# Five polynomial rounds instead of six, whole-tile ring places, one load for each slot

## The chip, the cores and the metric

The kernel runs on one core of one Trainium2 chip. The metric is the device time of one execution in microseconds (us). Three runs of the kernel before took 4946.76, 4948.24 and 4950.79 us, so the median is 4948.24 us.

## The reference: what is computed

The input `x` has 32 images of 64 channels and 56 by 56 = 3136 pixels. The work has two layers.

Layer 0 is a polynomial of the channels. The 64 channels are 8 groups of 8. In each group every product of two channels (36 of them) and of three channels (120) is formed at each pixel, and each set of products is mixed by a small matrix:

```
p2 = x[:, :, _I2] * x[:, :, _J2]
y2 = einsum('bgihw,goi->bgohw', p2, W2) + b2
p3 = x[:, :, _I3] * x[:, :, _J3] * x[:, :, _K3]
y3 = einsum('bgihw,goi->bgohw', p3, W3) + b3
return inp + y2 * beta2 + y3 * beta3 * 0.1
```

Layer 1 takes the result `l` of each image, `theta` being its first 32 channels. It forms the 3136 by 3136 matrix `theta^T theta`, takes a softmax of it along one axis and a second softmax of the result along the other, and multiplies this into `g = clip(bn(w_inside l), 0, 6)`. A 3 by 3 depthwise convolution, a normalization and the addition of `l` end the layer. Everything is float32.

## The kernel before, in words

**Layout.** The host reorders the channels so that the 32 rows of half an image (four groups) come as 8 planes of 4 rows, and appends the first five planes again behind the last. A load that begins `d` planes later therefore holds the channels turned by `d` places within each group. A product of channels `i`, `i+a`, `i+b` is the product of three loads with the offsets 0, `a`, `b`.

**Slots and rounds.** The 128 partitions are four slots of 32 rows. `STEPS` (line 51) says which offset `a` a slot has (slot 0 to 3: 0, 1, 2, 3) and with which `b` its products are extended. In round 0 GpSimd (POOL) forms `q = x0 * xa` for all slots at once; in rounds 1 to 4 it multiplies `q` by the tiles named `0`, `2`, `4` and `b`. TensorE (PE) multiplies each round's tile by its weights `wq[:, r]` and accumulates all rounds in PSUM. The fifth step, the pairs at offset 4, has no extension. It is a round of its own (round 5): POOL multiplies two small loads (`c`, offsets 0 and 4) of all four half images of a chunk in one instruction of 128 by 242, and PE multiplies that by a separate weight tile `w4`.

In the kernel before, the slot is the fast index of the partition (`wq[s::NSLOT]`, line 138), so one DMA with a plane step (`grow` in `LOADS`, line 216) fills all 128 partitions of one half image; only tile `b` needs two.

**Pairs, chunks and units.** Images go in 16 pairs. While the attention of pair `n` runs, the polynomial of pair `n+1` is made in 13 chunks of 242 pixels. A chunk of a pair has four half images (`ks`, four values of `k`). `products` (line 375) is a generator that emits a chunk's POOL instructions; it asks for room in two rings of products, `q` (8 places) and `pr` (20 places), and for loaded inputs. `load_next` and `prefetch` (lines 330 and 362) emit the loads in the order of a plan, as the rings `x0`, `xs` and `xc` have places and a credit of DMAs (`PACE`, line 305, given twice per attention tile) lasts. All loads of `x` behind the prologue are issued by SyncE (SP).

The second image of the first pair is made alone: chunks of two half images and 484 pixels (`TWO`). The first image of the first pair is made in a prologue of seven chunks of 448 pixels (`first_loads`, `first_products`, `first_poly`), where VectorE (DVE) does the multiplying and SP and ScalarE's queue (ACTq) issue the loads in turn.

**The attention's loop.** A pair has 49 tiles of 128 rows (`IT`). In loop step `t` PE makes the scores of tile `t` in two halves (`ps`, one PSUM buffer of four banks), DVE moves each half to SBUF and takes the row minimum (`e<-ps`), ACT makes two exponentials of 3136 columns, and PE multiplies tile `t-3` into the values (`av` and `ax<-gq,e`). The order on every engine is the order in which the program is written (`pin`, line 91). Between the halves there are places for other work, `aux0` and `aux1` for PE: units of the polynomial, each of two rounds (`rounds(..., 2)`, line 923), and units that make `g`. A chunk of a pair has three units, in `aux0` of three tiles that follow each other; `BETWEEN` (line 917) says where `g` units follow. `weight` and `split` divide the `av` products between a tile's two halves by the size of the units. After a chunk's last unit `poly_out` (line 493) adds the bias and `x` (the tile `xc`) on DVE.

## Time and profile before

| what | value |
|---|---|
| profiled execution: its span; the lowest time of the three runs | 4946.9 us; 4946.76 us |
| PE, ACT, DVE, POOL busy | 4722.0, 4553.9, 4120.5, 3208.4 us |
| one pair in the middle (from 3016.33 to 3309.82 us) | 293.49 us, 49 tiles |
| in that pair: PE, ACT, DVE, POOL busy | 287.90, 284.44, 255.94, 208.68 us |
| DMA in that pair | 0.57 of 16 engines, 145 GB/s |
| first exponential | at 124.44 us |

Times are microseconds unless marked ns. In the groups a line gives the engine, the operation, what it writes and reads, the shape and the count, then the busy time of the group, the mean of one instruction in ns, and the idle time ahead of them with what ended it. Every line number is that of a helper (L110), so tiles tell the groups apart. PE runs each float32 product in two passes, so a product is two records.

### The profile page before, as it was taken

What the parts mean: (1) busy time and instruction counts of PE and PEld (TensorE: products, weight loads), DVE (VectorE), ACT (ScalarE), POOL (GpSimd) and SP (SyncE); (2) the same over time, 40 slices, a digit from 0 to 9 for tenths busy, and PEclk for the clock granted to TensorE, in tenths of its full rate; (3) what the DMA queues carried; (4) which work ended last, traced back from release to release, by engine and by line L of the source; (5) the groups of instructions that cost most, each with busy time, mean ns of one, the idle gap of its engine ahead of it and who ended that gap; (6) DMA issues with size and microseconds to landing.
All of it is one profiled execution on the core that took longest, in us unless ns stands there. A gap on an engine that the chain in (4) does not pass through costs nothing.

```text
span 4946.9 us, 263995 instructions
## 1 busy us (share of the span) xinstructions
PE 4722.0 (95%) x118122; PEld 3215.6 (65%) x118122; DVE 4120.5 (83%) x6100; ACT 4553.9 (92%) x2356; POOL 3208.4 (65%) x4275
## 2 busy tenths in 40 slices
PE   4998999999999999999999999999999999999887
PEld 1555666666666666666666666666666666666665
DVE  4655898888988898888889889888888889888887
ACT  0777899999999999999999999999999999999996
POOL 1777685858758586785858768585875858678000
PEclk8999999999999999999999999999999999999999
DMA  6555656565565655556565555656555565554201
GB/s 203 152 148 153 146 144 155 145 151 141 138 145 145 152 147 143 147 145 144 149 145 147 147 146 142 150 145 152 146 140 141 150 147 146 145 147 125 45 11 34
DMA packets 875486, 685.65 MB, mean 139 GB/s; under 512 B 289772, under 2 KB 860524, under 8 KB 870252
## 3 DMA queue, kind: packets, MB, share of 16 engines
q1 hardware_dynamic: 865964, 657.85, 52.0%
q8 instruction: 924, 15.14, 1.3%
q10 hardware_dynamic: 8384, 10.91, 0.7%
q14 instruction: 214, 1.75, 0.1%
HBM read 565.65 MB, written 25.69 MB: 120 GB/s over the span
## 4 chain that ended last, share of the span: by engine, by line
PE 78%; DVE 11%; issue 3%; DMA 3%; ACT 3%; POOL 1%; SPq 1%; ACTq 0%; DVEq 0%; POOLq 0%
PE av L110 33%; PE ps L110 26%; PE ax L110 19%; DVE e L110 9%; ACT e L110 3%; DMA ring_xs<-in_x_dram 2%; POOL ring_pr L110 1%; DVE y L110 1%; DVE num L110 1%; SPq L110 1%; DMA ring_xc<-in_x_dram 1%; DMA first<-in_x_dram 1%; PE first_s L110 0%; DMA th<-y 0%; POOL ring_q L110 0%
## 5 line engine op out<-in xcount | busy, mean ns | idle before, releaser
L110 PEld LDWEIGHTS av<-gq,e 128*64 128x64 f32 x64512 | 2011.4, 138 | 943.1 <-issue 936.1
L110 ACT ACTIVATE e<-e,nm 128x3136 f32<-128x3136 f32 x784 | 2282.9, 2912 | 235.2 <-DVE e L110 219.6
L110 ACT ACTIVATE e<-e,rz 128x3136 f32<-128x3136 f32 x784 | 2270.3, 2896 | 0.0
L110 PE MATMUL av<-gq,e 128*64 128x65 f32 x64512 | 2224.2, 225 | 3.1 <-ACT e L110 3.0
L110 POOL TENSOR_TENSOR ring_pr<-ring_q,ring_xs 128x242 f32<-128x242 f32 (+2 forms) x2382 | 1784.5, 783 | 533.7 <-PE ax L110 522.8
L110 DVE TENSOR_SCALAR_CACHE_REDUCE e<-ps 128x1568 f32<-128x1568 f32 x784 | 1403.8, 1791 | 321.1 <-PE ps L110 301.7
L110 DVE TENSOR_SCALAR_CACHE_REDUCE e<-ps,nm 128x1568 f32<-128x1568 f32 x784 | 1448.3, 1847 | 254.1 <-PE ps L110 249.1
L110 PE MATMUL ps<-th 32*64 32x392 f32 x25088 | 1453.5, 515 | 131.6 <-DVE e L110 112.3
L110 POOL TENSOR_TENSOR ring_pr<-ring_q,ring_x 128x242 f32<-128x242 f32 (+2 forms) x794 | 606.2, 789 | 607.4 <-PE ax L110 574.8
L110 DVE SCALAR_TENSOR_TENSOR y<-tt,wdt,y 128x605 f32<-128x605 f32 (+6 forms) x711 | 708.2, 996 | 6.4 <-DMA tt<-tr 5.2
L110 PEld LDWEIGHTS ps<-th 32*64 32x64 f32 x25088 | 370.4, 130 | 476.8 <-DVE e L110 382.4
L110 POOL TENSOR_TENSOR ring_q<-ring_x,ring_xs 128x242 f32<-128x242 f32 (+2 forms) x794 | 570.3, 745 | 169.3 <-DMA ring_xs<-in_x_dram 166.4
L110 PE MATMUL ax<-gq,e 128*64 128x65 f32 x12288 | 490.3, 222 | 0.0
L110 PE MATMUL ax<-ring_pr,wq 128*32 128x242 f32 (+1 forms) x6448 | 474.5, 373 | 2.2 <-POOL ring_pr L110 1.1
L110 PEld LDWEIGHTS ax<-gq,e 128*64 128x64 f32 x12288 | 425.5, 138 | 0.3
L110 PEld LDWEIGHTS ax<-ring_pr,wq 128*32 128x32 f32 x6448 | 177.0, 109 | 106.9 <-POOL ring_pr L110 13.3
L110 POOL TENSOR_SCALAR y<-y,bias 128x616 f32<-128x616 f32 (+2 forms) x79 | 145.4, 1842 | 98.9 <-PE ax L110 98.9
L110 DVE SCALAR_TENSOR_TENSOR y<-ax,bias,ring_xc 128x242 f32<-128x242 f32 (+3 forms) x208 | 97.0, 467 | 102.6 <-PE ax L110 102.6
L110 PE MATMUL ax<-wit,y 128*64 128x64 f32 x3136 | 143.3, 223 | 31.1 <-issue 17.9
L110 POOL TENSOR_TENSOR ring_pr<-ring_xc 128x242 f32<-128x242 f32 (+3 forms) x208 | 127.7, 615 | 67.8 <-DMA ring_xc<-in_x_dram 59.2
L110 ACT ACTIVATION_READ_ACCUMULATOR e<-e,nm 128x1 f32 x784 | 145.4, 185 | 0.0
L110 PEld LDWEIGHTS ax<-wit,y 128*64 128x64 f32 x3136 | 118.9, 139 | 37.0 <-issue 18.7
(86 smaller groups left out, 1388.4 us busy)
## 6 DMA issues: line engine op xcount, KB each, us to landing
ring_xs<-in_x_dram SPq DMA_DIRECT2D x2184, 121.0 KB
ring_x<-in_x_dram SPq DMA_DIRECT2D x720, 121.0 KB
ring_xs<-in_x_dram SPq DMA_DIRECT2D x1440, 60.5 KB
th<-y SPq DMA_DIRECT2D x124, 392.0 KB
ring_xc<-in_x_dram SPq DMA_DIRECT2D x360, 121.0 KB
ring_xs<-in_x_dram SPq DMA_DIRECT2D x186, 116.0 KB
out_dram<-y SPq DMA_DIRECT2D x60, 308.0 KB
tt<-tr SPq DMA_DIRECT2D x128, 100.0 KB
```

Of the source, the lines that this page charges most:

```text
L110: i = f(*args, **kw)
```

## The change

- `STEPS` gets other extensions, so that round 1 multiplies `q` by the tile `a` itself (offsets 0 to 3), and slot 2 has nothing to do in round 2. Into that free slot go the pairs at offset 4: after the round's four products, four more POOL instructions of 32 partitions by 242 overwrite slot 2 with `x0 * x(offset 4)`. Round 5, `w4` and the second of the two `c` loads go. Five rounds stay; the third unit of a chunk holds one round instead of two.
- The slot becomes the slow index: slot `s` is partitions 32s to 32s+31. A tile of a chunk holds all half images of the chunk, and each of its four slots is filled by one DMA (`slot_loads`), 32 partitions by 4 half images by 242 columns.
- The rings hold whole tiles: `x0` 8 places instead of 6, `xs` 16 instead of 14, `xc` 2 of one load instead of 3 of two. Places come free a tile at a time. `PACE` goes from 4.5 to 4.
- POOL still multiplies one half image in each instruction (`pieces`).
- The prologue is changed in the same way; DVE does the extra slot there.

```
-    (0, [0, 2, 4, 5]),
-    (1, [0, 2, 4, 1]),
-    (2, [0, 2, 4, 5]),
-    (3, [0, 2, 4, 1]),
+    (0, [0, 2, 4, 1]),
+    (1, [1, 3, 4, 2]),
+    (2, [2, 4, 3]),
+    (3, [3, 5, 4, 0]),
     (4, []),
...
+SR, SS = 2, 2
...
     LOADS = {
-        "0": [(0, 1, 0, 0)],
-        "a": [(0, 1, 0, 1)],
-        "2": [(0, 1, 2, 0)],
-        "4": [(0, 1, 4, 0)],
-        "b": [(0, 2, 5, 0), (1, 2, 1, 0)],
+        "0": (0, 0, 0, 0),
+        "a": (0, 1, 2, 3),
+        "2": (2, 3, 4, 5),
+        "4": (4, 4, 4, 4),
+        "b": (1, 2, 3, 0),
     }
+    SPARE = slice(SS * 32, SS * 32 + 32)
+
+    def slot_loads(name, k0, nk, p0, w):
+        for s, d in enumerate(LOADS[name]):
+            yield slice(s * 32, s * 32 + 32), bass.AP(
+                x.tensor, (k0 * EXT + d) * 4 * N + p0, [[N, 32], [EXT * 4 * N, nk], [1, w]]
+            )
...
-    XB = {"x0": 6, "xs": 14, "xc": 3}
+    XB = {"x0": 8, "xs": 16, "xc": 2}
...
-    PACE = 4.5
+    PACE = 4
...
+        def times(dst, a, b):
+            for pc in pieces(ks):
+                pool.tensor_tensor(dst[:, pc, :], a[:, pc, :], b[:, pc, :], ALU.mult)
...
+        q = take_ring("q", w, nk)
+        times(q, x0, xa)
+        prefetch()
+        done(q)
+        for r, of in enumerate("a24b", 1):
+            yield "pr", m * nk
+            if of != "a":
+                yield "load", (n, c, ks, of)
+            xr = xa if of == "a" else use(of)
+            p = take_ring("pr", w, nk)
+            times(p, q, xr)
+            if r == SR:
+                times(p[SPARE], x0[SPARE], xr[SPARE])
+                held["x0"] -= m * nk
+            held["xs"] -= m * nk
             prefetch()
-                for r in range(0, NRND + 1, per)
+                for r in range(0, NRND, per)
```

More of the change, by code (lines that the diff above doesn't have):

```diff
@@ L132, in tile_poly_conv_attention @@
     wq = const.tile([128, NRND, 2, 32], FP, name="wq")
-    w4 = const.tile([128, 128], FP, name="w4")
     at = 0
     for s, (_, bs) in enumerate(STEPS):
-        for h in range(2) if s < NSLOT else ():
-            act.dma_start(
-                out=wq[s::NSLOT, :, h, :],
-                in_=wpoly[h * 32 : h * 32 + 32, at : at + NRND, h * 32 : h * 32 + 32],
-            )
-        if s == NSLOT:
-            act.dma_start(out=w4, in_=wpoly[:, at, :])
+        p0 = (s if s < NSLOT else SS) * 32
+        ranges = [(0, NRND, at)]
+        if s == SS:
+            ranges = [(0, SR, at), (SR + 1, NRND, at + SR)]
+        if s == NSLOT:
+            ranges = [(SR, SR + 1, at)]
+        for r0, r1, a in ranges:
+            for h in range(2):
+                act.dma_start(
+                    out=wq[p0 : p0 + 32, r0:r1, h, :],
+                    in_=wpoly[h * 32 : h * 32 + 32, a : a + r1 - r0, h * 32 : h * 32 + 32],
+                )
         at += 1 + len(bs)
@@ L160, in tile_poly_conv_attention @@
             out=ax[:, k * 256 : k * 256 + 256],
-            lhsT=w4,
+            lhsT=wq.rearrange("p k h o -> p (k h o)")[:, :128],
             rhs=wq.rearrange("p k h o -> p (k h o)")[:, :256],
@@ L204, in tile_poly_conv_attention @@
     firsts = [ep.tile([128, N], FP, name=f"first_{i}", tag="e") for i in range(4)]
-    def parts(tiles):
-        return [t[:, p : p + FW] for t in tiles for p, _ in FCS]
-    fx, fp = parts(firsts), parts(ys[1:] + [tt])
+    fx = [t[:, p : p + 2 * FW].rearrange("p (k w) -> p k w", k=2) for t in firsts for p, _ in FCS[:6:2]]
+    fc = [t[:C, 6 * FW :] for t in firsts]
+    fp = [t[:, p : p + FW] for t in ys[1:] + [tt] for p, _ in FCS]
     fat = {"x": 0, "p": 0, "q": 0, "c": 0}
@@ L216, in tile_poly_conv_attention, with load @@
     LOADS = {
-        "0": [(0, 1, 0, 0)],
-        "a": [(0, 1, 0, 1)],
-        "2": [(0, 1, 2, 0)],
-        "4": [(0, 1, 4, 0)],
-        "b": [(0, 2, 5, 0), (1, 2, 1, 0)],
-    }
+        "0": (0, 0, 0, 0),
[3 more added lines that the diff above has]
+        "b": (1, 2, 3, 0),
+    }
+    SPARE = slice(SS * 32, SS * 32 + 32)
[3 more added lines that the diff above has]
+                x.tensor, (k0 * EXT + d) * 4 * N + p0, [[N, 32], [EXT * 4 * N, nk], [1, w]]
+            )
     def first_loads(c):
         p0, w = FCS[c]
-        def load(dst, k, d, grow, steps):
-            src = bass.AP(x.tensor, (k * EXT + d) * 4 * N + p0, [[N, 32], [grow * 4 * N, steps], [1, w]])
-            if steps == 1:
-                src = bass.AP(x.tensor, (k * EXT + d) * 4 * N + p0, [[N, 32], [1, w]])
+        def load(dst, src):
             (act if fat["q"] % 2 else sync).dma_start(out=dst, in_=src)
@@ L234, in first_loads @@
         fxs[c] = {}
-        for name, k in [(a, k) for k in (0, 1) for a in "0a"] + [(a, k) for a in "24b" for k in (0, 1)]:
+        for name in "0a24b":
             t = fx[fat["x"] % len(fx)]
             fat["x"] += 1
-            fxs[c][name, k] = t
-            for s0, every, d, grow in LOADS[name]:
-                load(t[s0::every, :] if every > 1 else t, k, d, grow, NSLOT // every)
-        for d in (0, 1):
-            t = fx[fat["x"] % len(fx)]
-            fat["x"] += 1
-            fxs[c]["c", d] = t[:C, :]
-            for k in (0, 1):
-                load(t[k * 32 : k * 32 + 32, :], k, 4 * d, 0, 1)
+            for at, src in slot_loads(name, 0, 2, p0, w):
+                load(t[at], src)
+            for k in (0, 1):
+                fxs[c][name, k] = t[:, k, :]
+        t = fc[c % len(fc)]
+        fxs[c]["c"] = t
+        for k in (0, 1):
+            load(t[k * 32 : k * 32 + 32, :], bass.AP(x.tensor, k * EXT * 4 * N + p0, [[N, 32], [1, w]]))
     def first_products(c):
@@ L257, in first_products @@
         q = {k: product(xs["0", k], xs["a", k]) for k in (0, 1)}
-        frs[c] = [q] + [{k: product(q[k], xs[a, k]) for k in (0, 1)} for a in "024b"]
-        dve.tensor_tensor(xs["c", 1], xs["c", 0], xs["c", 1], ALU.mult)
-        frs[c].append(dict.fromkeys((0, 1), xs["c", 1]))
+        frs[c] = [q]
+        for r, a in enumerate("a24b", 1):
+            frs[c].append({})
+            for k in (0, 1):
+                p = product(q[k], xs[a, k])
+                if r == SR:
+                    dve.tensor_tensor(p[SPARE], xs["0", k][SPARE], xs[a, k][SPARE], ALU.mult)
+                frs[c][r][k] = p
     first_loads(0)
@@ L269, in tile_poly_conv_attention @@
     for k in range(NRND):
-        by = row("beta2_0") if k == 0 else b3row
-        w = wq[:, k, :, :].rearrange("p h o -> p (h o)")
-        dve.tensor_tensor(w, w, by, ALU.mult)
-    for half in (0, C):
-        w = w4[:, half : half + C]
-        dve.tensor_tensor(w, w, row("beta2_0"), ALU.mult)
+        cuts = [(slice(0, 128), row("beta2_0") if k == 0 else b3row)]
+        if k == SR:
+            cuts = [
+                (slice(0, SPARE.start), b3row),
+                (SPARE, row("beta2_0")),
+                (slice(SPARE.stop, 128), b3row),
+            ]
+        for at, by in cuts:
+            w = wq[at, k, :, :].rearrange("p h o -> p (h o)")
+            dve.tensor_tensor(w, w, by[at], ALU.mult)
     bias0 = const.tile([128, 1], FP, name="bias0")
@@ L313, in tile_poly_conv_attention @@
     ring = {t: [xp.tile([128, m, PCH], FP, name=f"ring_{t}", tag=t, bufs=1), 0] for t, m in XB.items() if t != "xc"}
-    ringc = xp.tile([128, 2 * XB["xc"] * PCH], FP, name="ring_xc", tag="xc", bufs=1)
+    ringc = xp.tile([128, XB["xc"] * PCH], FP, name="ring_xc", tag="xc", bufs=1)
     def chunks(ks):
@@ L320, in many, with pieces, take_ring @@
         return -(-w // PCH)
-    def take_ring(tag, w):
+    def pieces(ks):
+        return [slice(k, k + 1) for k in range(len(ks))]
+    def take_ring(tag, w, nk=1):
         t, at = ring[tag]
-        m, size = many(w), t.shape[1]
-        if at % m or at + m > size:
+        m, size = many(w) * nk, t.shape[1]
+        at = -(-at // m) * m
+        if at + m > size:
             at = 0
         ring[tag][1] = (at + m) % size
-        return t[:, at : at + m, :].rearrange("p m w -> p (m w)")[:, :w]
+        return t[:, at : at + m, :].rearrange("p (k m) w -> p k (m w)", k=nk)[:, :, :w]
     def load_next():
         tag, key = plan.pop(0)
-        n, c, ks, name, k = key
+        n, c, ks, name = key
         p0, w = chunks(ks)[c]
@@ L337, in load_next @@
             p0, w = p0 + sub * PCH, min(PCH, w - sub * PCH)
-            o = fat["c"] % XB["xc"] * 2 * PCH
+            o = fat["c"] % XB["xc"] * PCH
             fat["c"] += 1
-            t = ringc[:, o : o + 2 * PCH].rearrange("p (d w) -> p d w", d=2)
             at = slice(ks[0] * 32, ks[-1] * 32 + 32)
-            for d in range(2):
-                src = bass.AP(
-                    x.tensor,
-                    ((4 * n + ks[0]) * EXT + 4 * d) * 4 * N + p0,
-                    [[EXT * 4 * N, len(ks)], [N, 32], [1, w]],
-                )
-                start(t[at, d, :w], src)
-            loaded[key] = [t[at, d, :w] for d in range(2)]
-            return
-        held[tag] += many(w)
-        t = take_ring(tag, w)
-        for s0, every, d, grow in LOADS[name]:
             src = bass.AP(
                 x.tensor,
-                ((4 * n + k) * EXT + d) * 4 * N + p0,
-                [[N, 32], [grow * 4 * N, NSLOT // every], [1, w]],
-            )
-            start(t[s0::every, :] if every > 1 else t, src)
+                (4 * n + ks[0]) * EXT * 4 * N + p0,
+                [[EXT * 4 * N, len(ks)], [N, 32], [1, w]],
+            )
+            loaded[key] = ringc[at, o : o + w]
+            start(loaded[key], src)
+            return
+        held[tag] += many(w) * len(ks)
+        t = take_ring(tag, w, len(ks))
+        for at, src in slot_loads(name, 4 * n + ks[0], len(ks), p0, w):
+            start(t[at], src)
         loaded[key] = t
@@ L363, in prefetch @@
         while plan and credit[0] >= 1:
-            tag, (_, c, ks, _, _) = plan[0]
-            m = 1 if tag == "xc" else many(chunks(ks)[c][1])
+            tag, (_, c, ks, _) = plan[0]
+            m = 1 if tag == "xc" else many(chunks(ks)[c][1]) * len(ks)
             if held[tag] + m > XB[tag]:
@@ L380, in products @@
         p0, w = chunks(ks)[c]
-        m = many(w)
-        def use(name, k=None):
-            key = n, c, ks, name, k
-            return loaded.pop(key)
-        x0 = {}
-        rounds = [{}]
+        m, nk = many(w), len(ks)
+        rounds = []
         both = []
         prods[n, c, ks] = rounds, both
-        yield "q", m * len(ks)
-        for k in ks:
-            yield "load", (n, c, ks, "a", k)
-            x0[k] = use("0", k)
-            xa = use("a", k)
-            q = take_ring("q", w)
-            pool.tensor_tensor(q, x0[k], xa, ALU.mult)
-            rounds[0][k] = q
-            held["xs"] -= m
-            prefetch()
@@ L401, in products @@
-        for r, of in enumerate(("0", "2", "4", "b")):
-            rounds.append({})
-            yield "pr", m * len(ks)
-            for k in ks:
-                if of != "0":
-                    yield "load", (n, c, ks, of, k)
-                xr = x0[k] if of == "0" else use(of, k)
-                p = take_ring("pr", w)
-                pool.tensor_tensor(p, rounds[0][k], xr, ALU.mult)
-                rounds[-1][k] = p
-                held["x0" if of == "0" else "xs"] -= m
-                prefetch()
@@ L413, in products, with use, done @@
-        at = slice(ks[0] * 32, ks[-1] * 32 + 32)
-        yield "pr", m
-        p4 = take_ring("pr", w)[at, :]
+        def use(name):
+            return loaded.pop((n, c, ks, name))
+        def times(dst, a, b):
+            for pc in pieces(ks):
+                pool.tensor_tensor(dst[:, pc, :], a[:, pc, :], b[:, pc, :], ALU.mult)
+        def done(tile):
+            rounds.append({k: tile[:, i, :] for i, k in enumerate(ks)})
+        yield "q", m * nk
+        yield "load", (n, c, ks, "a")
@@ new lines, in products @@
+        x0, xa = use("0"), use("a")
+        q = take_ring("q", w, nk)
[9 more added lines that the diff above has]
+            times(p, q, xr)
+            if r == SR:
+                times(p[SPARE], x0[SPARE], xr[SPARE])
+                held["x0"] -= m * nk
+            held["xs"] -= m * nk
+            prefetch()
+            done(p)
@@ L416, in products @@
         for sub in range(m):
-            yield "load", (n, c, ks, f"c{sub}", None)
+            yield "load", (n, c, ks, f"c{sub}")
             both.append(use(f"c{sub}"))
-            pool.tensor_tensor(p4[:, sub * PCH : min((sub + 1) * PCH, w)], *both[sub], ALU.mult)
-        rounds.append({k: p4 for k in ks})
     feeds = []
@@ L447, in feed @@
     def feed(n, c, ks):
-        todo = [("x0" if name == "0" else "xs", name, k) for k in ks for name in "0a"]
-        for name in "24bc":
-            if name == "c":
-                todo += [("xc", f"c{sub}", None) for sub in range(many(chunks(ks)[c][1]))]
-            else:
-                todo += [("xs", name, k) for k in ks]
-        for tag, name, k in todo:
-            plan.append((tag, (n, c, ks, name, k)))
+        todo = [("x0" if name == "0" else "xs", name) for name in "0a24b"]
+        todo += [("xc", f"c{sub}") for sub in range(many(chunks(ks)[c][1]))]
+        for tag, name in todo:
+            plan.append((tag, (n, c, ks, name)))
         feeds.append((products(n, c, ks), None))
@@ L478, in poly @@
         rounds = prods[n, c, ks][0]
-        at = slice(ks[0] * 32, ks[-1] * 32 + 32)
         for r in rs:
@@ L483, in poly @@
                     out=ax[k * 32 : k * 32 + 32, AUX : AUX + w],
-                    lhsT=wq[:, r, k % 2, :] if r < NRND else w4[at, k * 32 : k * 32 + 32],
+                    lhsT=wq[:, r, k % 2, :],
                     rhs=rounds[r][k][:, px],
                     start=False,
-                    stop=(r == NRND),
+                    stop=(r == NRND - 1),
                     skip_group_check=True,
@@ L490, in poly @@
             if ends:
-                taken["pr" if r else "q"] -= (sub + 1) * (1 if r == NRND else len(ks))
+                taken["pr" if r else "q"] -= (sub + 1) * len(ks)
     def poly_out(n, c, ks, sub):
@@ L497, in poly_out @@
         assert n < 3 or all((n - 3, b) in stored for b in range(NB))
-        xc = prods[n, c, ks][1][sub][0]
+        xc = prods[n, c, ks][1][sub]
         held["xc"] -= 1
@@ L709, in make_diags @@
     def make_diags():
-        eye = take_ring("xs", 128)
+        eye = take_ring("xs", 128)[:, 0, :]
         pool.memset(eye, 0.0)
@@ L717, in make_diags @@
         for k in range(9):
-            t = take_ring("xs", 128)
+            t = take_ring("xs", 128)[:, 0, :]
             pool.tensor_scalar(t, eye, wdt[:, k : k + 1], None, ALU.mult)
@@ L801, in poly_unit @@
     def poly_unit(n, c, ks, rs, sub, hs):
-        ends = rs[-1] == NRND
+        ends = rs[-1] == NRND - 1
         unit(
@@ L833, in first_poly @@
         p0, w = FCS[c]
-        for r in range(NRND + 1):
+        for r in range(NRND):
             for k in (0, 1):
@@ L837, in first_poly @@
                     out=banks[c][k * 32 : k * 32 + 32, :w],
-                    lhsT=wq[:, r, k, :] if r < NRND else w4[:C, k * 32 : k * 32 + 32],
+                    lhsT=wq[:, r, k, :],
                     rhs=frs[c][r][k],
                     start=(r == 0),
-                    stop=(r == NRND),
+                    stop=(r == NRND - 1),
                     skip_group_check=True,
@@ L847, in first_out @@
         dve.scalar_tensor_tensor(
-            ys[0][:C, p0 : p0 + w], banks[c][:C, :w], bias0[:C], fxs[c]["c", 0], ALU.add, ALU.add
+            ys[0][:C, p0 : p0 + w], banks[c][:C, :w], bias0[:C], fxs[c]["c"], ALU.add, ALU.add
         )
@@ L924, in rounds @@
             return [
-                ("p", m, c, ks, list(range(r, r + per)), sub)
+                ("p", m, c, ks, list(range(r, min(r + per, NRND))), sub)
                 for sub in range(many(chunks(ks)[c][1]))
-                for r in range(0, NRND + 1, per)
+                for r in range(0, NRND, per)
             ]
```

## The prediction

> **What bounds the kernel now.** I read the page's engine totals first: PE is busy 95% of the span, ACT 92%, so a gain on PE alone may run into ACT. The averages hide stages, so I then read one pair in the middle, from ACT's timeline, the chain and the windows.

> ACT's timeline, the first exponentials of two neighbouring pairs:

> ```profile
> 3016.33 2.91 ACT L110 ACTIVATE e<-e,nm 128x3136 f32<-128x3136 f32 x1 [2.07 <-DVE e L110]
> 3309.82 2.91 ACT L110 ACTIVATE e<-e,nm 128x3136 f32<-128x3136 f32 x1 [2.07 <-DVE e L110]
> ```

> The same wait comes back after 293.49 us: a pair is 293.49/49 = 5.99 us a tile. The window of that stretch gives PE 287.90, ACT 284.44, DVE 255.94 and POOL 208.68 us busy. PE has 5.6 us of room, ACT 9.1 us (8.0 of it waits for DVE's `e`).

> The chain, two tiles of a chunk, those of its first and of its third unit:

> ```profile
> 2040.08 0.84 PE ps L110 x16
> 2040.92 1.08 PE av L110 x32
> 2042.01 0.95 PE ax L110 x16
> 2042.96 0.84 PE ps L110 x16
> 2043.80 1.67 PE av L110 x52
> 2045.47 0.47 PE ax L110 x16
> ...
> 2051.80 0.84 PE ps L110 x16
> 2052.64 1.32 PE av L110 x40
> 2053.95 0.95 PE ax L110 x16
> 2054.91 0.84 PE ps L110 x16
> 2055.75 1.43 PE av L110 x44
> 2057.18 0.82 PE ax L110 x28
> ```

> The 0.95 us is a unit of two rounds; the 0.82 us holds a `g` unit too. The tiles last 5.86, 5.86 (the one left out) and 6.20 us, together 17.92 us, with PE never idle. So in the poly stage PE sets the end, and the third tile of a chunk is the long one.

> The chain in a pair's light stretch, without polynomial:

> ```profile
> 3133.62 1.87 DVE e L110 x2
> 3135.49 0.04 issue
> 3135.53 1.00 PE ps L110 x16
> 3136.55 1.81 DVE e L110 x2
> ```

> Here scores and eviction follow each other through the single `ps` buffer: 2.93 + 2.88 = 5.81 us a tile. ACT's busy time says the same, 4553.9/784 = 5.81. Both are floors: a tile shorter on PE than about 5.82 gains nothing more.

> **The change: PE.** Round 5 goes:

> ```profile
> L110 PE MATMUL ax<-ring_pr,w 128*32 128x242 f32 x1440 | 107.7, 370 | 13.5 <-POOL ring_pr L110 13.5
> ```

> 1440 records are 180 chunks of 8, so 0.60 us busy each; half of the 0.95 us in the chain, 0.47, is what the path loses. The third tile falls from 6.20 to 5.73, under the floor of 5.82, so a chunk gains 0.38 us and not 0.47. A pair has 13 chunks; all but two (chunks 5 and 6) have a `g` unit behind the third unit, hence the long tile. The two others are near the floor already. Behind the shortened unit DVE still has `poly_out` (0.47), the bank's preparation (0.27 to 0.36) and the next eviction, in a half that now lasts 2.9 us; I leave 0.05 for that and take 0.33. 11 x 0.33 = 3.6 us a pair, in 14 steady pairs **51 us**. Ends: 0 (the floors take all) and 0.47 x 13 x 14 = 86 us.

> **POOL.** A chunk has 4 products for `q`, 16 for rounds and one `xc` product; it will have the 20 and four of 32 by 242.

> ```profile
> L110 POOL TENSOR_TENSOR ring_pr<-ring_q,ring_xs 128x242 f32<-128x242 f32 x2160 | 1604.0, 776 | 498.3 <-PE ax L110 488.5 <-DMA ring_xs<-in_x_dram 6.7 <-DMA ring_xc<-in_x_dram 2.7
> L110 POOL TENSOR_TENSOR ring_pr<-ring_xc 128x242 f32<-128x242 f32 x180 | 111.0, 617 | 57.4 <-DMA ring_xc<-in_x_dram 50.7 <-PE ax L110 5.8 <-PE ps L110 0.7
> ```

> No row shows 32 partitions. A 64-partition product took 616 ns and the 128-partition one 617, so partitions buy nothing there; I bound the new product by 0.617 and 0.776 and take 0.65, near the first, since it runs the same columns from tiles POOL has just read (zero is excluded by the 0.62 of the half-width form). A chunk goes from 4 x 0.742 + 4 x 0.783 + 12 x 0.776 + 0.617 = 16.0 us to 4 x 0.742 + 16 x 0.776 + 4 x 0.65 = 18.0 us (17.9 to 18.5), a pair gains 26 us of POOL work. What covers it: in the pair above POOL waits 76.5 us for PE to free a ring place (`ring_pr <- PE ax`), so about 50 stay. Where three-tile chunks follow each other (chunks 4 to 9, 17.6 us each) POOL loses 0.4 us a chunk plus two or three `y` additions of 1.83 us: some 8 us behind. A round's place is released four tiles (23 us) before PE needs the next chunk's product in it, and the work between is at most 6 us, so 8 is hidden, and the four-tile chunks give it back. Cost 0; if the cover is gone, PE waits for `ring_pr`.

> **Loads.** A chunk has 21 DMAs on SP instead of 26, and one `xc` load of 121 KB less, 1.6 MB of some 42 MB (145 GB/s x 293.49 us) a pair. A tile's product now waits for four DMAs and a place comes free per tile. A freed tile is needed again after at least three rounds, 4 + 4 + 4 products and the four small ones, 11 us; reloading it is four issues of about 0.6 us on SP, at worst behind four more for `x0` and one for `xc`, 5.4 us, and 2.4 to 5.3 us to land (the chain's `ring_xs` and `ring_xc` pieces). It fits by 0 to 3 us where POOL runs flat out, by far more elsewhere. `xc` waits in SP's queue for `poly_out` two chunks back, and `x0` and `a` of the next chunk stand behind it: two tiles ahead of their use. The SP queue is also passed by `th`, `tt` and the stores, as before. Cost 0.

> What is new is that each DMA fills 32 partitions. The nearest rows are the windows about the four `th` loads of 488 to 493, which also write 32 partitions each; the first window still holds 128-partition loads:

> ```profile
> 488.00:490.00 2.00, 2.00 (x64) 1.45 (x50) 1.27 (x1) 2.00 (x1) 1.38 (x3) 1.00 1.02 249
> 490.00:492.00 2.00, 0.29 (x10) 0.15 (x6) 0.67 (x3) 1.99 (x2) 0.00 (x0) 1.00 1.00 201
> ```

> The last two columns are the DMA engines' share and GB/s: saturated at 201 with narrow writes, against 249. The steady need of 41.0 MB in 289 us is 142 GB/s, and 2.6/17.6 + 24 = 172 in a dense chunk. It fits 201, at 0.7 to 0.86.

> [...]

> **The first pair.** (a) The prologue is bound by loads: the windows of 20 us from 20 to 40 and from 60 to 100 show 282, 255 and 251 GB/s at a share of 0.85 to 0.90. Its x is 16.8 MB instead of 17.7. At the old 255 that is 3 us less, at 201 it is 84 instead of 69 us, 15 more. Nearest are the prologue's own rows, yet the writes are narrow: I take +3. (b) Then comes this, in ACT's timeline:

> ```profile
> 87.09 30.52 ACTq L110 DMA_DIRECT2D th<-y  x8
> 124.44 2.91 ACT L110 ACTIVATE e<-e,nm 128x3136 f32<-128x3136 f32 x1 [5.46 <-DVE e L110]
> ```

> The `th` loads take until 117.6 to issue, though DVE had written the last `y` by 98.0: in the built order they share the rotating completion semaphores with `ring_x` loads that wait for POOL. In the built order of the changed kernel the loads ahead of them (`x0`, `a`, `2`, `4`, `b` of one chunk) have places and no POOL wait. `th` could land near 104 instead of 121; late next are those ring loads, now behind `th`. Gain 0 to 17, I take 11. (c) `TWO`: PE is busy without a break from 140 to 250, and 52 records of round 5 (7.8 us) go: 6 us, ends 0 and 8. (d) From 299 to 446 pair 1's chunks run one after another on POOL, 8 in 147 us, 18.4 each, with a 3.2 to 4.1 us wait for `ring_xc` ahead of each `xc` product. After: 20 x 0.68 + 4 x 0.62 = 16.1 us (means of that stretch), no such wait, 0 to 2 us for whole tiles; PE has 0.9 x 18.4 - 0.6 = 16 us of its own. I take 17.1, 1.3 x 10 chunks = 13 us; ends 0 and 23. DVE's extra prologue products (two of some 0.6 us for one) are hidden behind loads.

> Sum: 51 - 3 + 11 + 6 + 13 = 78 us. The profiled span of 4946.9 stands 1.3 under the median of 4948.24; 4948 - 78 = **4870 us**.

> **Rivals.**
> 1. The floors take it: the halves of the third tile wait for eviction as often as they gain, no steady gain. For it: 5.81 twice over, and DVE at 87% of the pair. Against: ACT's own 8.0 us of waits lie in the poly stage. Then only 78 - 51 = 27 go: 4921.
> 2. Slower: x loading becomes the bound, since 32-partition writes of 968-byte pieces are slower than `th`'s long ones. It decides when the rate at a full share falls under 142 GB/s. Against: 201. At 135 the 41.0 MB take 304 us a pair, 10 more in 15 pairs: 5100.
> 3. POOL becomes the bound: 24 products at over (293.5 - 9.2)/312 = 0.91 us. The mean is 0.776, and DVE's contending `y<-tt` steps barely change. Dense chunks alone would cost 2 us a pair at 0.83, eating half the gain: 4900.
> 4. The removal doesn't happen: excluded, the built order has five rounds.

> **How the numbers follow.** Forecast 0.66, its own range 4835 to 4905; rival 1 0.18; rival 2 0.10; rival 3 0.06. A measurement tells 0.2% (10 us) from no change. Forecast and rivals 1 and 3 are faster, but for rival 1 with a late prologue (15 us) too, 0.02 same and 0.02 slower: faster 0.86, same 0.02, slower 0.12. The range leaves out rival 2 and the lower tail where all upper ends meet (86 + 17 + 8 + 23): 4832 to 4932.

> **What would show it.** Right: no `ring_pr,w` group, pair period near 289.8, third tiles near 5.85, ACT's waits under 5 us a pair, first exponential near 116. Wrong: PE waiting for `ring_pr`, POOL for `ring_xs` by tens of us, a DMA share near 1, or a 32-by-242 product over 0.8 us.

## The result: slower, and the profile after

The changed kernel takes 5002.54 us in the median (4999.66 to 5018.64), the kernel before, beside it on the same chip, 4948.69 us. The ratio is 1.011, with a 95% interval from 1.0096 to 1.0128: 54 us slower, where 78 us faster was forecast. The profiled execution is one of the longer ones, 5018.64 us with a span of 5016.9 us, 70.0 us above the span of before.

ACT's timeline of the changed kernel: the `th` loads and the first exponential, and then the first exponentials of two neighbouring pairs. (The two lines of before in the prediction, 3016.33 and 3309.82 us, are called that too, but they are the 28th tiles of theirs, counted in steps of 49 tiles from 124.44 us; a pair's length is the same from either place: 293.44 us from first tile to first tile.)

```profile
87.91 18.12 ACTq L111 DMA_DIRECT2D th<-y  x8
114.64 2.91 ACT L111 ACTIVATE e<-e,nm 128x3136 f32<-128x3136 f32 x1 [7.30 <-DVE e L111]
...
2883.99 2.91 ACT L111 ACTIVATE e<-e,nm 128x3136 f32<-128x3136 f32 x1
3184.78 2.91 ACT L111 ACTIVATE e<-e,nm 128x3136 f32<-128x3136 f32 x1
```

The beginning went as forecast: the first exponential comes at 114.64 instead of 124.44 us. By the same timeline the tiles of pair 1 begin at 473.78 instead of 505.93 us, so 32.2 us are won there. The loss is in the steady pairs. This one lasts 300.79 us instead of 293.49, and the 14 of them 300.60 in the mean instead of 293.47: 7.13 x 14 = 99.8 us. Together 67.6 of the 70.0 us.

The window of that pair, with PE, PE's weight loads, DVE, ACT and POOL in this order, then the clock, the DMA share and GB/s:

```profile
2884.00:3184.80 300.80, 286.40 (x7284) 196.59 (x7285) 262.91 (x375) 284.43 (x148) 237.30 (x317) 0.99 0.59 137
```

PE has less to do (287.90 before), ACT the same, and the DMA engines are far from full. POOL has its 28.6 us more, but PE's products hardly wait for it in the whole run (us in total, times, longest):

```profile
PE ax L111 <- POOL ring_pr L111: 5.4, 15, 0.6
```

DVE has 7.0 us more (255.94 before), although no instruction of DVE was added to a pair (375 in both). The windows again, of the instructions that read `wdt` alone, give 46.43 us before and 54.27 after (DVE's time stands behind the comma):

```profile
3016.33:3309.82 293.49, 46.43 (x45) 0.00 (x0) 1.00 0.57 145
```

```profile
2884.00:3184.80 300.80, 54.27 (x45) 0.00 (x0) 0.99 0.59 137
```

The whole of DVE's increase, and a little more, lies in the depthwise convolution's steps, `y <- tt, wdt, y`, which the diff does not touch. All of them in the two kernels, with the shortest, middle and longest duration in ns, before and then after:

```profile
L110 DVE SCALAR_TENSOR_TENSOR y<-tt,wdt,y x711: 618/947/1434, 557.1 to 4941.4; 128x605 f32<-128x605 f32 x91, 128x616 f32<-128x616 f32 x45, 128x660 f32<-128x660 f32 x14, 128x672 f32<-128x672 f32 x8
```

```profile
L111 DVE SCALAR_TENSOR_TENSOR y<-tt,wdt,y x711: 619/902/9561, 524.7 to 5011.2; 128x605 f32<-128x605 f32 x91, 128x616 f32<-128x616 f32 x45, 128x660 f32<-128x660 f32 x14, 128x672 f32<-128x672 f32 x8
```

The middle one is even a little shorter, but the longest went from 1.43 to 9.56 us. Before, none of the 711 is above 1.5 us; after, 40 are, and 27 are above 2.5 us. One of them, in DVE's, POOL's and PE's timelines of the changed kernel:

```profile
2952.50 3.92 DVE L111 SCALAR_TENSOR_TENSOR y<-tt,wdt,y 128x605 f32<-128x605 f32 x1
2956.35 1.84 DVE L111 TENSOR_SCALAR_CACHE_REDUCE e<-ps,nm 128x1568 f32<-128x1568 f32 x1
```

```profile
2950.41 5.37 POOL L111 TENSOR_TENSOR ring_pr<-ring_q,ring_xs 128x242 f32<-128x242 f32 x8
2955.86 3.73 POOL L111 TENSOR_TENSOR ring_pr<-ring_x,ring_xs 32x242 f32<-32x242 f32 x4
```

```profile
2958.25 0.92 PE L111 MATMUL ps<-th 32*64 32x392 f32 x16 [2.56 <-DVE e L111]
```

The step begins 0.1 us after one of POOL's products and ends at 2956.42, after a run of eight products has ended and the first small product has begun. Its own work is 0.62 to 0.82 us by estimate (the shortest of the 711 steps took 0.62, the shortest of this shape 0.82), so it stands still for some 3.1 to 3.3 us. The next eviction starts behind it, and PE waits 2.56 us for that eviction, since `ps` is a single buffer. All 27 steps above 2.5 us end in this way, 0.56 to 0.58 us after the first of a chunk's four 32 by 242 products has begun. Many come back at the same place of one pair after the other: the five first ones of 3.9 us follow each other at 300 us.

The lengths of the pairs follow these standstills. What the steps last beyond 1.43 us, the longest of before, adds up to 7.0 us a pair in the mean of the 14 steady pairs. The pair with most of it (11.9 us, the step of 9.56 us is in it) lasts 307.12 us, the pair with least (3.8 us) 296.72.

The chain of waits shows the same tile (start, duration, what), and the third tile of its chunk:

```profile
2950.78 1.80 DVE e L111 x2
2952.58 0.06 DVE y L111
2952.64 3.71 issue
2956.35 1.86 DVE e L111 x2
...
2964.18 0.84 PE ps L111 x16
2965.03 1.55 PE av L111 x48
2966.58 0.55 PE ax L111 x8
2967.12 0.84 PE ps L111 x16
2967.97 1.20 PE av L111 x36
2969.16 0.82 PE ax L111 x28
```

The chain calls the standstill "issue", time in which it can name no cause, so the chain alone doesn't lead to POOL; the duration of the single step does. The last six pieces are a chunk's third tile without round 5: 0.55 where 0.95 stood, and 5.81 us from 2964.18 to 2969.99 instead of 6.20. The removal did what it was forecast to do, and the lock-outs (steps that stand still while POOL's products run) took back far more.

### The profile page after: what moved, and what is told of

It is laid out like the page before. It is cut to its first block, busy times and chain, and to the rows that moved or that the text cites. A ratio compares the mean times of both kernels' runs of the same rounds, so it can differ in the third digit from the quotient of the medians.

```text
span 5016.9 us, 256952 instructions
## 1 busy us (share of the span) xinstructions
PE 4676.7 (93%) x116482; PEld 3176.3 (63%) x116482; DVE 4224.1 (84%) x6107; ACT 4553.8 (91%) x2356; POOL 3649.2 (73%) x4861
## 4 chain that ended last, share of the span: by engine, by line
PE 65%; DVE 17%; issue 8%; DMA 4%; POOL 3%; ACT 3%; SPq 1%; ACTq 0%; POOLq 0%; DVEq 0%
PE av L111 27%; PE ps L111 24%; PE ax L111 14%; DVE e L111 13%; POOL ring_pr L111 3%; ACT e L111 3%; DVE y L111 2%; DMA ring_xs<-in_x_dram 2%; DMA first<-in_x_dram 1%; SPq L111 1%; DMA th<-y 0%; POOL ring_q L111 0%; DVE ax L111 0%; DVE tr L111 0%; DVE num L111 0%
## 5 line engine op out<-in xcount | busy, mean ns | idle before, releaser
L111 POOL TENSOR_TENSOR ring_pr<-ring_q,ring_xs 128x242 f32<-128x242 f32 (+2 forms) x3176 | 2311.9, 764 | 839.7 <-PE ax L111 760.0
L111 ACT ACTIVATE e<-e,nm 128x3136 f32<-128x3136 f32 x784 | 2282.8, 2912 | 314.8 <-DVE e L111 289.6
L111 PE MATMUL ps<-th 32*64 32x392 f32 x25088 | 1452.4, 517 | 245.8 <-DVE e L111 227.9
L111 DVE SCALAR_TENSOR_TENSOR y<-tt,wdt,y 128x605 f32<-128x605 f32 (+6 forms) x711 | 820.7, 1155 | 6.8 <-DMA tt<-tr 5.6
L111 PEld LDWEIGHTS ps<-th 32*64 32x64 f32 x25088 | 371.0, 130 | 607.5 <-DVE e L111 523.8
L111 POOL TENSOR_TENSOR ring_q<-ring_x,ring_xs 128x242 f32<-128x242 f32 (+2 forms) x794 | 555.6, 734 | 148.6 <-DMA ring_xs<-in_x_dram 148.6
L111 POOL TENSOR_TENSOR ring_pr<-ring_x,ring_xs 32x242 f32<-32x242 f32 (+2 forms) x794 | 643.2, 836 | 15.8
L111 PE MATMUL ax<-ring_pr,wq 128*32 128x242 f32 (+1 forms) x6448 | 497.7, 380 | 7.5 <-POOL ring_pr L111 5.4
L111 PE MATMUL ax<-ring_q,wq 128*32 128x242 f32 x1612 | 128.1, 380 | 0.1
```

The lines of the kernel that those rows point to most:

```text
L111: i = f(*args, **kw)
```

## Experiments

### Whose contention it is: POOL's runs, its load, DVE's operands

The explanation to test (A) is that a step with two operands in SBUF and POOL's products exclude each other, so that a run of products without a pause locks the step out. The rival (B) sees the cause elsewhere. The first kernel puts a one-column memset behind each product, to break the runs:

```
             for pc in pieces(ks):
                 pool.tensor_tensor(dst[:, pc, :], a[:, pc, :], b[:, pc, :], ALU.mult)
+                pool.memset(gap, 0.0)
```

> The changed kernel, with a POOL memset of one column of a scratch tile behind every product; nothing is left out. Theory A (VectorE's convolution steps, which read two operands in SBUF, are locked out while POOL's products follow each other without a break; the trace of the changed kernel shows steps of 3.9 to 9.6 us where the longest before was 1.43 us): the memsets give VectorE a place to get in, no step lasts over 1.6 us, a pair falls from 300.7 us to about 290 us and the time from 5003 to about 4885 us (4865 to 4910), although POOL works some 2 us more in each chunk. Rival B (POOL has too much work): more POOL work makes it slower, 5020 us or more. Rival C (loads into 32 partitions come late): the same time as the changed kernel, about 5000 us.

Measured: 4951.5 us in the median (4924.39 to 4970.52), ratio to before 1.000 (0.998 to 1.002). That is 51 of the 133 us between the changed kernel and its forecast of 4870, though POOL has 477 us more to do, and B's 5020 us or more is wrong; but A's number is missed too. In the profiled execution 19 steps are above 1.5 us, the longest 7.79 us: breaks of this kind help, but don't let every step in.

The second leaves out the four small products, and with them the pairs at offset 4:

```
             if r == SR:
-                times(p[SPARE], x0[SPARE], xr[SPARE])
                 held["x0"] -= m * nk
```

> The changed kernel without the four products of 32 partitions (the pairs at offset 4 are left out, slot 2 of round 2 keeps a product that belongs to nothing). POOL has 2.7 us less work in each chunk. Theory A: the wait ahead of these four is one of the places where POOL's run is broken, so steps of 3.9 us and more stay or become longer; 4980 to 5060 us. Rival B: a lighter POOL than with the products, 4900 us or less. Rival C: about 5000 us.

Measured: 4840.34 us (4836.88 to 4851.3), ratio 0.978 (0.977 to 0.980). Here A as first put is wrong: whole-tile waits and products in fours stay, and only 2 steps are above 1.5 us (3.80 and 4.73). Without the four small products POOL waits 1139 us for PE's ring places instead of 695 (by the 128 by 242 groups of `ring_pr`). So the load that they bring belongs to the cause, as B has it.

The third takes the second SBUF operand from DVE's steps; a control, run with the next group, does the same in the kernel before:

```
-        dve.scalar_tensor_tensor(
+        dve.tensor_scalar(
...
-            yr,
+            None,
...
-            ALU.add,
+            ALU.min,
+            accum_out=acc1,
```

> The changed kernel, with the convolution step on VectorE as a product of one SBUF operand by a column (the accumulation into y is left out, so the convolution is not computed; a step writes a row minimum beside it). Theory A: a step with one operand in SBUF isn't locked out, none lasts over 1.2 us; a pair is near 289 us, the time near 4870 us (4840 to 4900), what the prediction gave. Rivals B and C: PE waits for products or products for loads as now, 4980 us or more.

> The control to the changed kernel with one-operand steps: the kernel before with the convolution's steps as tensor_scalar, one SBUF operand and accum_out; the accumulation over the nine taps is left out, so the output isn't the reference's. Theory A: in the kernel before the lock-outs are short (1.43 us at most) and PE sets the end, so little changes: 4935 to 4950 us, and the difference to the changed kernel's 4869 is then the gain that the prediction worked out, 65 to 80 us, without the contention. Rival B (one-operand steps speed up any version, since DVE becomes lighter): 4870 to 4900 us, and the change is worth little even without the contention.

Measured: the changed kernel with one-operand steps takes 4869.38 us (4868.63 to 4871.28), ratio 0.984 (0.982 to 0.986); the kernel before with them 4950.49 us (4945.2 to 4953.17), ratio 1.000 (0.999 to 1.001). The steps of the first:

```profile
L111 DVE TENSOR_SCALAR_CACHE_REDUCE y<-tt,wdt x711: 612/837/908, 520.7 to 4861.2; 128x605 f32<-128x605 f32 x91, 128x616 f32<-128x616 f32 x45, 128x660 f32<-128x660 f32 x14, 128x672 f32<-128x672 f32 x8
```

None is above 0.91 us, and POOL's products, just as many, run beside them. That is A's number. This pair of runs settles where the loss is: without a second SBUF operand on DVE the change is worth 81 us (77 when each of the two is set against the kernel before on its own chip), with it minus 54, and the kernel before doesn't care.

The last of this group is the kernel before with the waits for loads taken ahead of each round, by four one-column copies on POOL, so that the products behind them wait for no load:

```
+            if of != "0":
+                yield "load", (n, c, ks, of, ks[-1])
+                for k in ks:
+                    pool.tensor_copy(early, loaded[n, c, ks, of, k][:, :1])
```

> The kernel before, with four POOL copies of one column ahead of the four products of rounds 2, 3 and 4, each reading one of the loaded tiles: the copies take the waits for the DMAs, and the four products behind them have a wait for PE alone, as in the changed kernel. Nothing else is changed. Theory A in the form that the waits for DMAs between products are what let VectorE in: some steps last over 1.6 us, up to four products (about 3.5 us), and the time rises by 5 to 60 us over 4948 us. If the waits have nothing to do with it: no step over 1.5 us and 4945 to 4955 us, POOL having 76 us of slack in each pair for the copies.

Measured: 4973.56 us (4969.29 to 4974.99), ratio 1.005 (1.003 to 1.006). Nine steps above 1.5 us, up to 3.28 us, where the kernel before has none. All nine end 0.7 us after one of the copies has begun. Step and time lie where A in this form had them, but the copies are also 534 us more work for POOL (busy 74% of the span instead of 65%), so this run does not tell the missing waits from the load.

### Load alone, and longer instructions

Theory A now said that POOL's load moves its products out of step with DVE. So the load was put into the kernel before:

```
+            if r == 2:
+                for k in ks:
+                    pool.tensor_tensor(extra[64:96, :w], rounds[0][k][64:96], rounds[0][k][64:96], ALU.mult)
```

> The kernel before with four more POOL products of 32 by 242 in each chunk, behind the four of round 2; they read a product of round 0 twice and write a scratch tile that nothing reads, so the output is the reference's and PE, the loads and the rings stay as before. Theory A (POOL's load moves its products out of step with DVE, and the two-operand convolution steps are locked out): 2.7 us more POOL work a chunk makes lock-outs of several us as in the changed kernel, 50 to 160 us slower than before, 5000 to 5110 us, the longest step over 5 us. Rival B (the lock-outs need the changed kernel's layout, where a product waits for a whole tile of four DMAs and then runs without a break): the extra products vanish in POOL's waits for ring places, 4945 to 4965 us, the longest step under 3.5 us.

Measured: 4971.81 us (4966.79 to 4991.71), ratio 1.005 (1.003 to 1.007). POOL is busy 74% of the span, as in the changed kernel (73%), and one step of 711 is above 1.5 us, at 5.53 us. Both theories missed the time: load alone costs less than A said, and a little more than B allowed. Steps above 1.5 us are thus none in the kernel before, 1 with more load alone, 2 with the changed layout and no more load (the second kernel above; POOL is busy 63% of the span there and 65% in the kernel before) and 40 with both: the many lock-outs need the load together with something in the changed kernel's layout. That this something is the fours without a pause is argued, not shown.

Next, fewer and longer instructions of POOL, two and four half images in each:

```
-        return [slice(k, k + 1) for k in range(len(ks))]
+        return [slice(k, k + 2) for k in range(0, len(ks), 2)]    # or [slice(0, len(ks))]
```

The rival to A here (C, not the one of the first kernel) is that a longer product keeps a step out for longer: 4990 us or more with either.

> The changed kernel with POOL multiplying two half images, 484 columns, in each instruction (the pieces of a chunk are slices of two); nothing else. Theory A: POOL's work falls to 10 products of some 1.25 us and two small ones, 15 us a chunk, less than the 16.0 of before, so POOL waits for PE again and the lock-outs are few: 4850 to 4890 us. [...]

> The changed kernel with POOL multiplying all four half images of a tile, 968 columns, in one instruction; nothing else. Theory A: POOL's work is 14.5 us a chunk or less, but a step that loses against one instruction waits up to 2.4 us: 4850 to 4900 us, the longest step some 3.5 us. Rival C: steps locked out for whole instructions, most of them over 2 us, 4990 us or more.

Measured: two, 4911.06 us (4905.56 to 4911.98), ratio 0.992 (0.990 to 0.993); four, 5095.12 us (5085.76 to 5114.14), ratio 1.030 (1.027 to 1.032). With two, 105 steps are above 1.5 us but only 2 above 2.5; with four, 119 are above 2.5 us, the longest 5.10: a 968-column product lasts 2.25 us where no step runs beside it. Neither theory had the first number: POOL's load fell as A said, yet a product that a step loses to lasts 1.22 us instead of 0.71. With four the rival was right, and A wrong.

### A pause on POOL

The longest lock-outs of the changed kernel ended where a POOL instruction had to wait for POOL's own result: the first small product overwrites a slot that the products ahead of it have written. A2, a narrower form of A, says that a step gets in only where POOL's next product is held back. Its rival L says that POOL's load alone decides. A drain holds it back without other work (in the run with one ahead of every product these follow each other every 0.86 us instead of 0.66):

```
             for pc in pieces(ks):
+                pool.drain()                     # ahead of every product
...
+                if pc.start == 2:                # or: ahead of the third of four
+                    pool.drain()
```

> The changed kernel with a drain on POOL ahead of every product (4764 of them): each product starts only when the one before it has ended; nothing else. Theory A2 (a two-operand step of DVE gets its turn only where POOL's next product is held back, by a separate wait instruction ahead of it or by a wait for POOL's own result; in the changed kernel 34% of the products have a separate wait ahead, in the kernel before 50%, and the steps that were locked out all end at the first 32 by 242 product, which waits for POOL): no step above 1.5 us, and the gain of the shorter third tiles comes back, 4860 to 4900 us. Rival L (POOL's load alone decides; the drains add some 0.1 us each, 2.4 us a chunk, to it): as slow as the changed kernel or slower, 5000 us or more, with steps of several us.

> The changed kernel with one drain on POOL in each tile of four products, ahead of the third (1166 drains); nothing else. Theory A2: a step that is locked out waits for four products at most, some 3.3 us with its own time, instead of up to thirteen; most of the gain comes back, 4870 to 4930 us. Rival L: a quarter of the drains' load of the run with a drain ahead of every product, so the changed kernel's time within 15 us, 4990 to 5020 us.

Measured: with a drain ahead of every product 5412.22 us (5408.38 to 5415.19), ratio 1.093 (1.091 to 1.095); one in each tile of four, 4898.31 us (4897.6 to 4898.98), ratio 0.989 (0.988 to 0.990). The steps of both, the drain everywhere first:

```profile
L111 DVE SCALAR_TENSOR_TENSOR y<-tt,wdt,y x711: 619/909/1399, 602.8 to 5400.9; 128x605 f32<-128x605 f32 x91, 128x616 f32<-128x616 f32 x45, 128x660 f32<-128x660 f32 x14, 128x672 f32<-128x672 f32 x8
```

```profile
L111 DVE SCALAR_TENSOR_TENSOR y<-tt,wdt,y x711: 620/940/1409, 540.0 to 4891.5; 128x605 f32<-128x605 f32 x91, 128x616 f32<-128x616 f32 x45, 128x660 f32<-128x660 f32 x14, 128x672 f32<-128x672 f32 x8
```

In both no step is above 1.41 us, less than the 3.3 us that A2 allowed in the second: the lock-outs are gone. The time of the first was missed all the same, for the drains cost more than I put them at. Products that followed each other every 0.66 us now follow every 0.86, and the chain of waits of that kernel, its shares by engine, says what bounds it:

```profile
POOLq 36%; PE 30%; issue 12%; DMA 9%; DVE 6%; SPq 4%; ACT 2%; POOL 1%; ACTq 0%; DVEq 0%
```

POOL's own sequencer leads with 36%. With one drain in four the load fits, and the time is A2's, not L's. The steady pairs then take 290.98 us in the mean, against 300.60 without the drains, although POOL has more to do. Of these 9.6 us, 8.0 are the convolution's steps themselves (46.2 us a pair against 54.2). Of what this kernel waits for:

```profile
PEld ps L111 <- DVE e L111: 418.8, 966, 3.3
ACT e L111 <- DVE e L111: 160.0, 114, 8.4
PE ps L111 <- DVE e L111: 128.4, 298, 2.0
```

The changed kernel had 523.8, 289.6 and 227.9 us in these three lines, and its longest waits were 8.8, 9.1 and 8.3 us.

> The changed kernel with products of two half images (484 columns) and a drain on POOL ahead of each (2382 drains). The same without drains took 4911 us, with 105 steps of 1.5 to 4 us. Theory A2: a step loses one product of 1.2 us at most, so steps of up to 1.95 us stay and the longer ones go: 4890 to 4912 us. Rival L: the drains' load of some 1.2 us a chunk comes on top, 4911 to 4940 us.

> The kernel before with a drain on POOL ahead of every product of the rings: the control to the changed kernel with drains. Theory A2: the steps of before are 1.43 us at most and one-operand steps in their place changed nothing (4950 us), so drains give nothing either: 4940 to 4955 us; a gain of the drained changed kernel is then not one that drains bring to any kernel. Rival (drains help by themselves, since POOL and DVE always contend): 4900 us or less.

Measured: products of two half images with drains, 4981.03 us (4980.88 to 4982.26), ratio 1.006 (1.004 to 1.007); the kernel before with drains, 5051.85 us (5045.08 to 5053.31), ratio 1.020 (1.018 to 1.021). The control shows that drains ahead of every product don't speed up a kernel that has no lock-outs; one drain in four was not tried in the kernel before. The control missed A2's number, as the drains cost more here too: POOL's sequencer has 20% of its chain. The run with two half images missed both numbers: no step is above 1.95 us, as A2 said, but 158 are above 1.5 us and the middle one is 1.32 us instead of 0.86. Why so many more steps then meet a product is open.

### The order of the small products, and the first pair apart

The same instructions in another order, each small product directly behind the product whose slot it overwrites, so that POOL waits for its own result sooner and more often:

```
-            times(p, q, xr)
-            if r == SR:
-                times(p[SPARE], x0[SPARE], xr[SPARE])
+            times(p, q, xr, x0 if r == SR else None)   # the small product inside the loop
```

> The changed kernel with each 32 by 242 product directly behind the product whose slot it overwrites, instead of all four behind the four; the same instructions, another order. Each small product waits for POOL's own result, so round 2 has four such waits instead of one, the first of them three products earlier. Theory A2: a step locked out in the rounds ahead gets in up to 2 us sooner, and none is locked out within round 2: the longest step falls from 9.6 to some 4 us, and the time to 4930 to 4980 us. Rival L (POOL's load decides): the changed kernel's time, 4995 to 5015 us.

Measured: 4975.47 us (4967.93 to 4993.63), ratio 1.004 (1.003 to 1.006). As A2 said, it is 27 us better than the changed kernel with nothing added or left out, and the longest step falls from 9.56 to 4.81 us. There are not fewer long steps, though: 31 are above 2.5 us instead of 27, and 22 of them end just after a small product has begun.

Last, long products for the chunks made in the first pair, where there are no convolution steps and POOL sets the pace, and one drain in four products afterwards:

```
-            for pc in pieces(ks):
+            for pc in pieces(ks, 2 if n < 2 else 1):
+                if n > 1 and pc.start == 2:
+                    pool.drain()
```

> The changed kernel with products of two half images (484 columns) for the chunks made in the first pair, where POOL is the bound, and products of one half image with a drain ahead of the third of each tile from then on. Theory A2 with the first pair's cost as a separate term: pair 1's tiles begin near 446 us, as in the run with 484 columns everywhere, instead of 489 in the run with one drain a tile, and the steady pairs take 290.8 us as there: 4898 - 43 = 4855 us, 4845 to 4870. Rival (the two are not separate, e.g. the steady pairs lose their rhythm when the first pair ends elsewhere): 4890 us or more.

Measured: 4861.34 us (4860.01 to 4866.16), ratio 0.982 (0.980 to 0.983): the fastest complete version here. Its pair 1 begins at 451.29 us, against 488.98 with one drain in four throughout, and its steady pairs take 290.89 us. The 37.0 us between the two runs' medians are the 37.7 us of the first pair.

## Why the prediction was wrong, point by point

- **PE, 51 us: right, a little too large.** The group `ring_pr,w` is gone, and the third tile fell to 5.81 us, the floor named. Between the two kernels with one-operand steps the steady pairs went from 293.38 to 290.27 us in the mean: 3.1 us a pair instead of 3.6, 0.28 us a chunk instead of 0.33, 43.6 us in all. The removal of round 5 works as the prediction has it; 0.33 us a chunk was a little too much.
- **First pair, 27 us: right.** The first exponential came 9.8 us sooner (8 forecast), pair 1 began 32.2 us sooner. The prologue's narrow loads ran at 244, 218 and 222 GB/s in the three windows that had shown 282, 255 and 251: slower, as the 3 us taken off allowed for, but above the 201 that the prediction took for the worst case.
- **Loads, cost 0: right.** The pair moves 137 GB/s at a share of 0.59, by estimate 137/0.59 = 232 at a full share, above the 201 of the `th` loads; and ahead of the 128 by 242 products of `ring_q` POOL waits 40.4 us for loads in the whole run, against 66.1 before. Rival 2 falls with that.
- **POOL, cost 0: the step that failed.** Its sizes were roughly right. The small product takes 0.70 us where nothing contends with it (the run with one-operand steps), against 0.65 taken, and 0.835 in the changed kernel, above the 0.8 that the prediction had named as a sign of being wrong: DVE gets in there, at the first of four above all (0.97 us in the mean, the other three 0.79). And the cover was there: PE waits 5.4 us for `ring_pr` in the whole run. But the step asked only whether PE would wait for POOL. The price is paid by a third engine: rival 3's sentence that "DVE's contending `y<-tt` steps barely change" took a mean of before (0.996 us, and 1.43 at most) for a property of the instruction. It held in the kernel before, where half of POOL's products have a wait ahead of them. With a fuller POOL and products that wait for a whole tile instead of each for its own load, single steps stand still for up to 9.56 us and pass it on through the single `ps` buffer: the steps take 8.0 us more a pair than with one drain in four, and a pair 9.6 us more.
- **Range.** It had no case in which the contention grows. All bounds on POOL's cost were taken from how long its products last, none from how long it can keep another engine out.

The sum of 78 us is what the change is worth without that: 81 us between the medians of the two kernels with one-operand steps; in their profiled spans 76.3 us, of which 32.6 are the first pair and 43.6 the steady ones. That the sum fits so closely is in part luck: the steady pairs gave 7 us less than the forecast's 51, the first pair 6 more than its 27.

What the prediction left out is the number of SBUF operands: beside POOL's products a DVE step with two of them lasted up to 9.56 us in the changed kernel, a step with one 0.91 us at most. No run ahead of the prediction compared the two; that the steps of 128x605 took anything from 0.82 to 1.39 us in the kernel before was a hint at most. And a step can lose to more than the one product that it meets: the longest lost to a run of thirteen products and the rest of the one that it met, which fits (9.56 - 0.62) / 0.66 = 13.5.

## What to carry to other kernels

When work is added to an engine that has time to spare, ask not only who waits for its results but whose instructions last longer beside it: count the pauses that the added work fills. Look at the longest of a group's instructions, not at its mean, since lock-outs of 4 to 6 us, about two in a pair, moved the mean of 711 steps by 0.16 us only, and in the chain of waits carried no name. And a pause that looks useless can be what lets another engine in: one drain in four products, with POOL doing more, won over 100 us (4898.31 against 5002.54).
